# Score tiles of the four-block attention units: one accumulation chain in one pair of PSUM banks instead of two

## The chip, the cores and the metric

The kernel runs on one core of a Trainium2 chip. The metric is the device time of one execution in microseconds (us), as the median of several runs. Matmuls run on TensorE (PE, with weight loads as PEld), the other engines are VectorE (DVE), ScalarE (ACT), GpSimd (POOL) and SyncE (SP, which here issues the DMAs).

## The reference

One transformer block on x of 2 x 1024 tokens of width 512, with a modulation from a small conditioning vector. Cut to what matters here, for attention:

```python
h = _layernorm(x, axis=-1) * (1 + ca) + sa
q = (h @ Wq)   # 32 heads of 64, rotary embedding applied
k = (h @ Wk)   # 8 heads of 64, rotary embedding applied; each serves 4 query heads
v = (h @ Wv)   # 8 heads of 64
scores = einsum('bhqd,bhkd->bhqk', q, k) / sqrt(64)
scores = where(causal, scores, finfo.min)
out = einsum('bhqk,bhkd->bhqd', softmax(scores), v)
x = x + ga * (out @ Wo)
```

After it comes a second layernorm with modulation and a gated feed-forward of width 2048 with ternary weights and an RMS norm in the middle; the output is the residual sum. All arrays are float32.

## The kernel before

The kernel has four stages: projections of keys, values and queries with the rotary embedding (up to about 300 us in the profile), attention (to about 1030 us), the output projection with the second norm, and the feed-forward. To keep float32 accuracy on faster matmuls, an operand is split into a high and a low part, and a product is three matmul terms: high by high, high by low, low by high.

Attention goes by units. A unit (b, g, i) is one batch, one key head with its four query heads, and one group of 256 query rows, i from 0 to 3. There are 64 of them, and a unit has nb = 2i + 2 key blocks of 128 keys: 2, 4, 6 or 8. For each unit:

- "tops": `top_mm` multiplies queries by keys (high parts alone) into a pair of PSUM banks (`pm`), and `top_red` on DVE takes each query row's maximum (`mx`, with `mm` for the first half of long rows). The maxima go through `top_row` into `rows`.
- `score(j)`: the scores of key block j, transposed (keys on partitions), for four heads, in two halves of the PE array's rows. Each half writes a bank of its own, so a score tile takes a pair of banks (`ps_`). A block that starts a chain takes four terms: three products and one matmul of `unit` by `rows`, which subtracts the maximum. The next block of the chain doesn't start anew: it adds the products with the *step* of the keys, k[j] - k[j-1], onto the banks that still hold the scores of block j-1; three terms and no row term. It may do so only when both exponentials of block j-1 have read the banks (`es[j - 1]` among the task's `after`).
- `expo(j, half)`: ACT writes the exponentials into `e`; `causal(j)` on POOL masks the last two blocks.
- `value(j)`: PE multiplies `e` by the values into `po`. Values run in tasks of `SPAN[nb]` blocks.
- `total` on POOL or DVE adds the `e` tiles up (`acc`), `row_sum` sums over keys on PE (`pr`), and the result is inverted and multiplied in.

Keys are stored in DRAM in `ks`, their steps' high parts in `kds`; `load_k` and `load_steps` bring them into the tiles k1, k2 and k3. In `ks` the place of the low part holds, for key blocks 0 and 4, the low part of the block itself, and for the others the low part of the step. `FIRST` says which blocks start a chain, `ORDER` the order in which a unit's blocks are scored:

```python
ORDER = {2: [0, 1], 4: [0, 2, 1, 3], 6: [0, 4, 1, 5, 2, 3], 8: [0, 4, 1, 5, 2, 6, 3, 7]}
FIRST = {2: [0], 4: [0, 2], 6: [0, 4], 8: [0, 4]}
```

So a unit of four has two chains, 0-1 and 2-3, each in a pair of banks. Since block 2 starts a chain only in the units of four (in the longer units it is a step), its own low part is kept in an extra place of 128 columns at the front of `kds` and k3.

The order of the instructions on each engine is worked out when the program is built. Every piece is a task with a cost, a due time and what it waits for (`add`), and `Plan.run` lays them out one by one with a model of engines, banks and buffers. For PE it chooses among the tasks that can start now by due time, with corrections: `STICK` favours a task of the class PE is in (the classes are the tiling modes: full array, column-tiled values and row sums, row-tiled scores and tops); `LATE` puts off a task whose inputs are only just ready; a top is favoured by `BOOST` when DVE has less than `FEED` us of work ahead and put off by `DELAY` when it has more than `ENOUGH`; and when PE would leave the score class while DVE has less than `FILL` us of work ahead, a top is taken instead if one can start:

```python
key=lambda o: (o[2].due - STICK * (CLASS[o[2].mode] == CLASS[mode]) + LATE * o[1] - (o[2].feeds > 0) * (BOOST * (behind < FEED) - DELAY * (behind > ENOUGH)), o[2].n))
if mode == 3 and best[2].mode != 3 and behind < FILL:
    best = min((o for o in opts if o[0] <= start + TURN and o[2].feeds > 0), key=lambda o: (o[2].due, o[2].n), default=best)
```

`LATE` also enters the choice on the other engines. The eight PSUM banks are given out by the planner: two to each chain of scores, two to each pair of tops, one to a unit's `po`, and one each to short products. The weights' ternary quantisation (`pq` on PE, `ws`, `wr` on DVE) is spread over the attention stage as filling. In the first stage, `rope_mul` and `rope_end` form the steps of the keys and write them.

Of the kernel before, what the change touches and what calls it, by code (L numbers as in the profile page):

```python
# [9 lines left out]
F32R = mybir.dt.float32r  # L10
BF = mybir.dt.bfloat16
AF = mybir.ActivationFunctionType
ALU = mybir.AluOpType
# [4 lines left out]
B, S, E = 2, 1024, 512  # L18
# [162 lines left out]
TBEG, TEND, PER_UNIT = 300, 20.0, 0.8  # L181
VSUM, VSIGN, LAST = 9, 1, 3
TBEFORE, TGAP, TSKIP = 20, 20.0, 25.0
LEAD, SPREAD, STICK, LATE = 15, 0.6, 9, 4
ENTER, LEAVE, LOAD, AHEAD = 0.16, 0.37, 0.1, 0.25
CLASS = (0, 1, 1, 2)
TURN, SPARE = 0.05, 1.0
FEED, BOOST, ENOUGH, DELAY, FILL = 0.3, 22, 2, 8, 3.5
QT, PACE = 6, 4

@with_exitstack
def block_kernel(ctx, tc, x, wq, wk, wv, wo, wgu, wpj, cin, wmod, cos, sin, out):
    nc = tc.nc
    T = InOrder(tc, nc.tensor, True)
    V, A, P, SY = (InOrder(tc, e, False) for e in (nc.vector, nc.scalar, nc.gpsimd, nc.sync))
# [3 lines left out]
    def f32(ap):  # L199
        return ap.bitcast(F32)  # L200

    const = ctx.enter_context(tc.tile_pool(name="const", bufs=1, reuse_waits="tile"))
    dram = ctx.enter_context(tc.tile_pool(name="dram", bufs=1, space=DRAM))
# [7 lines left out]
    def stile(name):  # L211
        if plan:
            return bank(plan.given.pop(0), name)
        turn_of["s"] += 1
        return bank(turn_of["s"] % 4, name)
# [30 lines left out]

    qs = [[dram.tile([128, 2, 2, S], F32R, name=f"qs{b}_{g}") for g in range(KVH)] for b in range(B)]
    ks = [[dram.tile([128, 4, S], F32R, name=f"ks{b}_{i}") for i in range(2)] for b in range(B)]
    kds = [[dram.tile([2, 128, S // 8 * 7], F32R, name=f"kds{b}_{i}") for i in range(2)] for b in range(B)]
    vs = dram.tile([NT, KVH * D], F32, name="vs")  # L250

    def put_q(dst, rr, h, tok):
# [130 lines left out]
    first = {}  # L383
# [84 lines left out]
    def rope_end(n):  # L468
        while len(ropes) > n:
            (a, c, *steps), tok, dst = ropes.pop(0)  # L470
            rr = tp.tile([128, 4, 512], F32R, name="rr")
            for i, r in enumerate((a, c)):
                A.activation(rr[:, i, :], r, AF.Copy)
                if not steps:
                    V.tensor_tensor(rr[:, 2 + i, :], r, f32(rr[:, i, :]), ALU.subtract)
                    continue
                V.tensor_tensor(rr[:, 2 + i, 0:128], r[:, 0:128], f32(rr[:, i, 0:128]), ALU.subtract)
                f, to = (128, 512) if tok else (0, 0)
                if not tok:

                    V.tensor_tensor(r[:, 0:128].bitcast(F32R), r[:, 256:384], f32(rr[:, i, 256:384]), ALU.subtract)
                high = r[:, 128:512].bitcast(F32R)
                A.activation(high, steps[i], AF.Copy)
                V.tensor_tensor(rr[:, 2 + i, 128:512], steps[i], f32(high), ALU.subtract)
                half = [x for pair in kds for x in pair][[x for pair in ks for x in pair].index(dst)][i]
                SY.dma_start(f32(half[:, to:to + 512 - f]), f32(r[:, f:512].bitcast(F32R)))
            for h in (0, 2, 1, 3):
                if len(dst.shape) == 4:
                    put_q(dst, rr, h, tok)
                else:  # L490
                    SY.dma_start(f32(dst[:, h, tok:tok + 512]).rearrange("(c d) t -> d c t", c=4), f32(rr[h * 32:h * 32 + 32]))
# [92 lines left out]
    hs = []  # L584
# [33 lines left out]
    def pe(n):  # L618
        return n / 2400 + 0.018
# [19 lines left out]
    for g in range(KVH):  # L639
        d, due = {}, 5.2 * g  # L640
# [118 lines left out]

    B0 = 5.2 * KVH  # L760

    ORDER = {2: [0, 1], 4: [0, 2, 1, 3], 6: [0, 4, 1, 5, 2, 3], 8: [0, 4, 1, 5, 2, 6, 3, 7]}
    FIRST = {2: [0], 4: [0, 2], 6: [0, 4], 8: [0, 4]}
    due_s, t = {}, B0
    for u, (b, g, i) in enumerate(units):
        nb = 2 * i + 2
        for j in ORDER[nb]:
            due_s[(u, j)] = t
            n = 128 if j == nb - 1 else 256
            t += (3 + (j in FIRST[nb])) * pe(2 * n) + 8 * n / 2400 + 0.05  # L770
            t += (4 * sum((2 * i + s + 1) * 128 / 2400 + 0.06 for s in range(2)) + PER_UNIT) / nb
        due_s[(u, nb)] = t
    PBEG = t
# [11 lines left out]
    def attention(u):  # L785
        b, g, i = units[u]
# [14 lines left out]
        if u % NI == 0:  # L801
            kd = K[(b, g)] = {}

            def load_k(n):
                l, a = n // 2, n % 2
                if a == 0:
                    kd["k", l] = kp.tile([128, S], F32R, name=("k1", "k2")[l])
                SY.dma_start(f32(kd["k", l][a * 64:a * 64 + 64, :]), f32(ks[b][g // 4][l * 64:l * 64 + 64, g % 4, :]))

            def load_v():  # L810
                kd["vt"] = kp.tile([128, S // 128, 128], F32, name="vt")
                SY.dma_start(kd["vt"], vs[b * S:(b + 1) * S, g * 64:g * 64 + 128].rearrange("(t p) n -> p t n", p=128))

            kd["l"], before = [], K[units[u - 1][:2]]["l"] if u else []
            def load_steps(n):
                if n == 0:
                    kd["k", 2] = pp.tile([128, S // 8 * 7], F32R, name="k3", bufs=2)
                p = n % 2 * 64 + n // 2 * 32
                SY.dma_start(f32(kd["k", 2][p:p + 32, :]), f32(kds[b][g // 4][n // 2, g % 4 * 32:g % 4 * 32 + 32, :]))

            for n in range(4):
                kd["l"].append(add("S", 0.46, t0 - 26 + n, lambda n=n: load_k(n), order=kd["l"] + (held or before),
                                   takes=(("k1",), (), ("k2",), ())[n], dma=256 * KB))
            for n in range(4):
                kd["l"].append(add("S", 0.46, t0 - 22 + n, lambda n=n: load_steps(n), order=kd["l"], takes=() if n else ("k3",), dma=96 * KB))
            if g % 2 == 0:
                kd["lv"] = add("S", 0.46, t0 - 15, load_v, order=held or (K[units[u - 8][:2]]["lv"],) if u >= 8 else (), takes=("vt",), dma=512 * KB)
                kd["av"] = []
            else:
                kd["lv"] = K[(b, g - 1)]["lv"]  # L830
                kd["av"] = K[(b, g - 1)]["av"]
            kd["use"] = []
# [69 lines left out]

        def score(j):
            q0 = 128 if j == nb - 1 else 0
            first = j in FIRST[nb]
            c = max(x for x in FIRST[nb] if x <= j)
            if first:
                for hp_ in range(2):
                    d["p", c, hp_] = stile("ps_").rearrange("p (b q) -> p b q", q=256)
                ws = [kd["k", l][:, j * 128:(j + 1) * 128] for l in (0, 0)] + [kd["k", 2][:, 0:128] if j == 2 else kd["k", 1][:, j * 128:(j + 1) * 128]]  # L910
            else:
                at = j - j // 4
                ws = [kd["k", 2][:, at * 128:(at + 1) * 128]] * 2 + [kd["k", 1][:, j * 128:(j + 1) * 128]]
            terms = [(w_, d["t"][:, l]) for w_, l in zip(ws, (0, 1, 0))] + [(unit, rows[u % 2])] * first
            for n, (w_, x_) in enumerate(terms):
                for hp_ in range(2):
                    r = slice(hp_ * 64, hp_ * 64 + 64)
                    T.matmul(d["p", c, hp_][:, :, q0:], w_[r], x_[r, :, q0:], start=(n == 0 and first), stop=(n == len(terms) - 1), skip_group_check=True)

        def expo(j, hp_):  # L920
            q0 = 128 if j == nb - 1 else 0
            hs = slice(hp_ * 2, hp_ * 2 + 2)
            if hp_ == 0:
                home, tag, bufs = (gp, "eb", EL) if late_e[u, j] else (pp, "e", EB)
                d["e", j] = home.tile([128, 4, 256], F32, name="e", tag=tag, bufs=bufs)
            A.activation(d["e", j][:, hs, q0:], d["p", max(x for x in FIRST[nb] if x <= j), hp_][:, :, q0:], AF.Exp, scale=0.125)

        def causal(j):
            q0 = 128 if j == nb - 1 else 0
# [27 lines left out]
        for at, j in enumerate(order):  # L957
            n = 128 if j == nb - 1 else 256
            due = due_s[(u, j)]
            es[j] = []  # L960
            first, c = j in FIRST[nb], max(x for x in FIRST[nb] if x <= j)
            p = add("T", (3 + first) * pe(2 * n) + 0.03, due, lambda j=j: score(j), d["lq"] + kd["l"] + [row] + (cleared[1:2] if u == 0 else []) + ([] if first else es[j - 1]),
                    takes=("#", "#1") if first else (), mode=3)
            if first:
                chain[c] = p
            if late_e[u, j] or (u, j) not in early:
                p.order(opened)
            kd["use"].append(p)
# [1 line left out]
            for hp_ in range(2):  # L970
                x_ = add("A", ac(2 * n), due + 0.5 + 0.5 * hp_, lambda j=j, h=hp_: expo(j, h), (p,), order=es[j],
                         takes=() if hp_ else ("eb",) if late_e[u, j] else ("e",))
                if late_e[u, j]:
                    x_.order(opened)
                if j + 1 in FIRST[nb] or j == nb - 1:
                    chain[c].hold(("#", "#1")[hp_], x_)
                es[j].append(x_)
            ex[j] = es[j]
            if j >= nb - 2:
# [653 lines left out]
```

## Time and profile before

| | us |
|---|---|
| median of 3 runs | 1593.22 |
| lowest and highest | 1592.65, 1593.77 |
| the profiled execution | 1593.43 |
| its span in the profile | 1591.7 |

Busy time of the engines in three stretches of the span, in us:

| stretch | PE | DVE | ACT | POOL | granted clock | DMA share |
|---|---|---|---|---|---|---|
| 0 to 300 (projections) | 284.1 | 240.1 | 91.8 | 161.1 | 0.97 | 0.72 |
| 300 to 1030 (attention) | 708.7 | 593.6 | 408.9 | 478.8 | 0.99 | 0.55 |
| 1030 to 1592 (output projection, feed-forward) | 552.9 | 331.4 | 205.3 | 223.4 | 1.00 | 0.40 |

The stretches are cut by eye; tasks of neighbouring stages overlap. A matmul's end is modelled in the profile, so that records of neighbouring matmuls overlap: a busy PE need not be PE at its peak. All instructions carry the line of a helper (L39), so they are told apart by the names of what they write and read: `ps__7260<-t,k` is a score matmul into the score tile 7260, `ps__...<-row,unit` its row term, `pm` a top, `po` a value, `pr` a row sum, `pq` a ternary sum. A value or row-sum matmul (float32 operands) is recorded as two instructions.

### The profile page before, as it was taken

The numbers are of one execution on the slowest core, as the hardware profiler recorded it, in microseconds if no ns is written. First come the engines' busy times: TensorE is split into PE (matmuls) and PEld (weight loads), VectorE is DVE, ScalarE is ACT, GpSimd is POOL, SyncE is SP. The second block draws the span as 40 slices with busy tenths as digits, with TensorE's granted clock in tenths as the row PEclk, the third lists the DMA queues.
The fourth block names the chain that finished last, engine by engine and source line by source line (L and its number), as shares of the span: only waits on it lengthen the run. The fifth ranks groups of instructions, "written<-read, shape, count | busy, mean of one in ns | idle before, by whom it ended". The sixth has DMA issues, their size and how long they took to land.

```text
span 1591.7 us, 26776 instructions
## 1 busy us (share of the span) xinstructions
PE 1545.7 (97%) x9028; PEld 1068.5 (67%) x9028; DVE 1165.1 (73%) x2456; ACT 706.0 (44%) x1361; POOL 863.3 (54%) x764
## 2 busy tenths in 40 slices
PE   8899999999999999999999999999999999999998
PEld 7688887755554555555555555477787887888886
DVE  6798887787777788887878888847878675444434
ACT  3423222246555556555545656635555432222221
POOL 4365565537676676655676675713323544444443
PEclk9999999989999999999999999999999999999999
DMA  7766758775555445655546554576868733020000
GB/s 244 231 198 194 230 166 233 225 190 140 159 153 158 139 126 171 170 138 157 155 133 172 144 150 143 161 245 206 249 213 248 283 109 130 1 80 0 14 14 27
DMA packets 206593, 250.55 MB, mean 157 GB/s; under 512 B 34932, under 2 KB 144500, under 8 KB 206456
## 3 DMA queue, kind: packets, MB, share of 16 engines
q1 hardware_dynamic: 206456, 248.85, 52.6%
q8 instruction: 71, 1.16, 0.3%
q14 instruction: 66, 0.54, 0.1%
HBM read 156.24 MB, written 92.02 MB: 156 GB/s over the span
## 4 chain that ended last, share of the span: by engine, by line
PE 66%; DVE 6%; DMA 5%; issue 2%; SPq 2%; ACT 1%; POOL 1%; DVEq 0%; POOLq 0%; ACTq 0%
PE pgu L39 15%; PE po L39 13%; PE pj L39 10%; PE pfo L39 7%; PE pm L39 4%; DVE junk L39 3%; PE pr L39 3%; PE pqk L39 3%; SPq L39 2%; DMA k<-ks 2%; DMA t<-qs 1%; DVE mm L39 1%; ACT e L39 1%; PE pq L39 1%; DMA ri<-linv 1%
## 5 line engine op out<-in xcount | busy, mean ns | idle before, releaser
L39 POOL TENSOR_TENSOR acc<-acc,e 128x512 f32<-128x512 f32 x202 | 265.6, 1326 | 62.6 <-DVE acc L39 44.8
L39 PE MATMUL po<-e,vt 128*64 128x512 f32 (+1 forms) x1280 | 267.8, 557 | 4.1 <-DVE mx L39 1.8
L39 PE MATMUL pgu<-h,gu 128*128 128x512 f32 x1024 | 244.3, 391 | 0.0
L39 PEld LDWEIGHTS pgu<-h,gu 128*128 128x128 f32 x1024 | 192.0, 188 | 39.8
L39 DVE CUSTOM_DVE_ANT_0 junk<-pm,cmask,mm 128x384 bf16<-128x384 f32 (+1 forms) x256 | 174.6, 682 | 59.6 <-PE pm L39 34.7
L39 PEld LDWEIGHTS po<-e,vt 128*64 128x64 f32 x1280 | 84.0, 136 | 154.0 <-issue 122.2
L39 PE MATMUL pm<-k,t 64*128 64x384 f32 (+3 forms) x768 | 167.0, 385 | 13.6 <-DVE mx L39 5.3
L39 POOL TENSOR_SCALAR_AFFINE_SELECT e<-e 128x512 f32<-128x512 f32 x128 | 87.6, 687 | 144.7 <-ACT e L39 144.0
L39 PEld LDWEIGHTS pm<-k,t 64*128 64x128 f32 x768 | 94.1, 187 | 103.0 <-issue 31.3
L39 POOL TENSOR_TENSOR s<-hm 128x512 f32<-128x512 f32 x59 | 68.8, 1165 | 163.0 <-DVE hm L39 162.9
L39 DVE CUSTOM_DVE_ANT_0 junk<-pm,cmask 128x128 bf16<-128x128 f32 (+3 forms) x256 | 124.6, 487 | 37.8 <-PE pm L39 15.0
L39 DVE TENSOR_REDUCE mm<-pm 128x1 f32<-128x384 f32 (+2 forms) x256 | 128.4, 546 | 30.0 <-PE pm L39 29.7
L39 PE MATMUL pj<-woH,oh 128*128 128x512 f32 x512 | 142.1, 399 | 0.0
L39 POOL TENSOR_TENSOR on<-on,ri 128x512 f32<-128x512 f32 x64 | 85.8, 1342 | 65.9 <-DMA ri<-linv 65.4
L39 DVE TENSOR_TENSOR mL<-hm,mH 128x512 fp32r<-128x512 f32 x64 | 76.1, 1189 | 60.7 <-ACT mH L39 60.7
L39 DVE TENSOR_TENSOR hm<-gs,pgu 128x512 f32<-128x512 f32 x64 | 43.9, 685 | 94.1 <-PE pgu L39 89.7
L39 PEld LDWEIGHTS pj<-woH,oh 128*128 128x128 f32 x512 | 95.1, 188 | 20.9 <-issue 2.3
L39 ACT ACTIVATE mH<-hm 128x512 fp32r<-128x512 f32 x64 | 40.4, 632 | 146.0 <-PE pfo L39 133.2
L39 POOL TENSOR_TENSOR ra<-ra,rb 128x512 f32<-128x512 f32 x40 | 51.7, 1294 | 89.7 <-DVE rb L39 80.1
L39 PE MATMUL pfo<-pj,mH 128*128 128x512 f32 x256 | 100.4, 392 | 0.0
L39 PE MATMUL pfo<-pj,mL 128*128 128x512 f32 x256 | 99.7, 389 | 0.0
L39 ACT ACTIVATE on<-po 128x512 f32<-128x512 f32 x64 | 38.2, 597 | 102.5 <-POOL acc L39 44.3
(1488 smaller groups left out, 3707.8 us busy)
## 6 DMA issues: line engine op xcount, KB each, us to landing
qs<-rr SPq DMA_DIRECT2D x128, 256.0 KB
t<-qs SPq DMA_DIRECT2D x64, 512.0 KB
k<-ks SPq DMA_DIRECT2D x64, 256.0 KB
ri<-linv SPq DMA_DIRECT2D x128, 128.0 KB
os<-on SPq DMA_DIRECT2D x64, 256.0 KB
ks<-rr SPq DMA_DIRECT2D x32, 256.0 KB
w<-in_wgu SPq DMA_DIRECT2D x32, 256.0 KB
gus<-wr SPq DMA_DIRECT2D x32, 256.0 KB
```

The costliest lines, as they stand in the source:

```text
L39: ins = f(*a, **k)
```

## The change

In units of four blocks the second chain goes: blocks 0, 1, 2 and 3 are scored in this order and add up in one pair of banks; block 2 is a step like any other and has no row term. The units of two, six and eight keep their chains. With that, the extra place of block 2's low part goes from `kds` and k3 (7/8 of S columns become 3/4), as do the eight subtracts in `rope_end` that filled it. Four numbers of the planner change as well: STICK, LATE, FEED and FILL.

```diff
-LEAD, SPREAD, STICK, LATE = 15, 0.6, 9, 4
+LEAD, SPREAD, STICK, LATE = 15, 0.6, 6, 2
-FEED, BOOST, ENOUGH, DELAY, FILL = 0.3, 22, 2, 8, 3.5
+FEED, BOOST, ENOUGH, DELAY, FILL = 0.6, 22, 2, 8, 1
...
-    kds = [[dram.tile([2, 128, S // 8 * 7], F32R, name=f"kds{b}_{i}") for i in range(2)] for b in range(B)]
+    kds = [[dram.tile([2, 128, S // 4 * 3], F32R, name=f"kds{b}_{i}") for i in range(2)] for b in range(B)]
...
-                f, to = (128, 512) if tok else (0, 0)
-                if not tok:
-
-                    V.tensor_tensor(r[:, 0:128].bitcast(F32R), r[:, 256:384], f32(rr[:, i, 256:384]), ALU.subtract)
...
-                SY.dma_start(f32(half[:, to:to + 512 - f]), f32(r[:, f:512].bitcast(F32R)))
+                SY.dma_start(f32(half[:, tok // 4 * 3:tok // 4 * 3 + 384]), f32(high))
...
-    ORDER = {2: [0, 1], 4: [0, 2, 1, 3], 6: [0, 4, 1, 5, 2, 3], 8: [0, 4, 1, 5, 2, 6, 3, 7]}
-    FIRST = {2: [0], 4: [0, 2], 6: [0, 4], 8: [0, 4]}
+    ORDER = {2: [0, 1], 4: [0, 1, 2, 3], 6: [0, 4, 1, 5, 2, 3], 8: [0, 4, 1, 5, 2, 6, 3, 7]}
...
-            first = j in FIRST[nb]
-            c = max(x for x in FIRST[nb] if x <= j)
-            if first:
+            if j % 4 == 0:
                 for hp_ in range(2):
-                    d["p", c, hp_] = stile("ps_").rearrange("p (b q) -> p b q", q=256)
-                ws = [kd["k", l][:, j * 128:(j + 1) * 128] for l in (0, 0)] + [kd["k", 2][:, 0:128] if j == 2 else kd["k", 1][:, j * 128:(j + 1) * 128]]
+                    d["p", j // 4, hp_] = stile("ps_").rearrange("p (b q) -> p b q", q=256)
+                ws = [kd["k", l][:, j * 128:(j + 1) * 128] for l in (0, 0, 1)]
             else:
-                at = j - j // 4
+                at = j - 1 - j // 4
...
-                if j + 1 in FIRST[nb] or j == nb - 1:
-                    chain[c].hold(("#", "#1")[hp_], x_)
+                if j % 4 == 3 or j == nb - 1:
+                    chain[j // 4].hold(("#", "#1")[hp_], x_)
```

The left-out lines of the diff make the same replacement of `FIRST` by `j % 4` in the due times, in `expo` and where the score tasks are added, and the size of k3.

More of the change, by code (lines that the diff above doesn't have):

```diff
@@ L769, in block_kernel @@
             n = 128 if j == nb - 1 else 256
-            t += (3 + (j in FIRST[nb])) * pe(2 * n) + 8 * n / 2400 + 0.05
+            t += (3 + (j % 4 == 0)) * pe(2 * n) + 8 * n / 2400 + 0.05
             t += (4 * sum((2 * i + s + 1) * 128 / 2400 + 0.06 for s in range(2)) + PER_UNIT) / nb
@@ L816, in load_steps @@
                 if n == 0:
-                    kd["k", 2] = pp.tile([128, S // 8 * 7], F32R, name="k3", bufs=2)
+                    kd["k", 2] = pp.tile([128, S // 4 * 3], F32R, name="k3", bufs=2)
                 p = n % 2 * 64 + n // 2 * 32
@@ L904, in score @@
             q0 = 128 if j == nb - 1 else 0
-            first = j in FIRST[nb]
-            c = max(x for x in FIRST[nb] if x <= j)
-            if first:
+            if j % 4 == 0:
                 for hp_ in range(2):
-                    d["p", c, hp_] = stile("ps_").rearrange("p (b q) -> p b q", q=256)
-                ws = [kd["k", l][:, j * 128:(j + 1) * 128] for l in (0, 0)] + [kd["k", 2][:, 0:128] if j == 2 else kd["k", 1][:, j * 128:(j + 1) * 128]]
+                    d["p", j // 4, hp_] = stile("ps_").rearrange("p (b q) -> p b q", q=256)
+                ws = [kd["k", l][:, j * 128:(j + 1) * 128] for l in (0, 0, 1)]
             else:
-                at = j - j // 4
+                at = j - 1 - j // 4
                 ws = [kd["k", 2][:, at * 128:(at + 1) * 128]] * 2 + [kd["k", 1][:, j * 128:(j + 1) * 128]]
-            terms = [(w_, d["t"][:, l]) for w_, l in zip(ws, (0, 1, 0))] + [(unit, rows[u % 2])] * first
+            terms = [(w_, d["t"][:, l]) for w_, l in zip(ws, (0, 1, 0))] + [(unit, rows[u % 2])] * (j % 4 == 0)
             for n, (w_, x_) in enumerate(terms):
@@ L917, in score @@
                     r = slice(hp_ * 64, hp_ * 64 + 64)
-                    T.matmul(d["p", c, hp_][:, :, q0:], w_[r], x_[r, :, q0:], start=(n == 0 and first), stop=(n == len(terms) - 1), skip_group_check=True)
+                    T.matmul(d["p", j // 4, hp_][:, :, q0:], w_[r], x_[r, :, q0:], start=(n == 0 and j % 4 == 0), stop=(n == len(terms) - 1), skip_group_check=True)
         def expo(j, hp_):
@@ L925, in expo @@
                 d["e", j] = home.tile([128, 4, 256], F32, name="e", tag=tag, bufs=bufs)
-            A.activation(d["e", j][:, hs, q0:], d["p", max(x for x in FIRST[nb] if x <= j), hp_][:, :, q0:], AF.Exp, scale=0.125)
+            A.activation(d["e", j][:, hs, q0:], d["p", j // 4, hp_][:, :, q0:], AF.Exp, scale=0.125)
         def causal(j):
@@ L960, in attention @@
             es[j] = []
-            first, c = j in FIRST[nb], max(x for x in FIRST[nb] if x <= j)
+            first = j % 4 == 0
             p = add("T", (3 + first) * pe(2 * n) + 0.03, due, lambda j=j: score(j), d["lq"] + kd["l"] + [row] + (cleared[1:2] if u == 0 else []) + ([] if first else es[j - 1]),
@@ L964, in attention @@
             if first:
-                chain[c] = p
+                chain[j // 4] = p
             if late_e[u, j] or (u, j) not in early:
```

## The prediction

> **What bounds the kernel now.** I read the page's head first, then the busy time by stage, then the PE queue in order of time through the attention stage, then the waits.
>
> ```profile
> span 1591.7 us, 26776 instructions
> PE 1545.7 (97%) x9028; PEld 1068.5 (67%) x9028; DVE 1165.1 (73%) x2456; ACT 706.0 (44%) x1361; POOL 863.3 (54%) x764
> PE 66%; DVE 6%; DMA 5%; issue 2%; SPq 2%; ACT 1%; POOL 1%; DVEq 0%; POOLq 0%; ACTq 0%
> ```
> ```profile
> 300.00:1030.00 730.00, 708.65 (x5213) 393.63 (x5211) 593.61 (x1612) 408.89 (x844) 478.78 (x431) 0.99 0.55 155
> ```
>
> The columns of the second fence are the stretch, then busy time of PE, PEld, DVE, ACT, POOL, the granted clock, the DMA share and GB/s. PE ends the kernel (66% of the chain), and in the attention stage, 300 to 1030 us, it looks 97% busy while DVE is at 594 of 730 us and DMA at 55%. But the end of a matmul's record is modelled (0.39 us for 512 columns), so I counted by starts. Back to back, a pair of 64x512 score matmuls (the two halves run side by side) starts every 0.23 us (638.77 to 639.00 below; 0.2275 over longer runs); sixteen value records take 3.16 us (631.58 to 634.74), 0.1975 each; eight row-sum records take 0.46 us. With these prices the stage's records come to 286 us of scores and tops, 226 of values, 53 of row sums and 17 of full-array matmuls, 582 of 730 us. So about 148 us of the stage is PE time lost between instructions, some 105 of them in the 131 stretches of scores and tops. The change works on that pool, and on the 582.
>
> ```profile
> 629.82 0.49 PE L39 MATMUL ps__7260<-t,k 64*128 64x512 f32 x1
> ...
> 630.62 0.39 PE L39 MATMUL ps__7260<-row,unit 64*128 64x512 f32 x1
> ...
> 630.85 0.80 PE L39 MATMUL pm<-k,t 64*128 64x384 f32 x2
> 631.58 3.23 PE L39 MATMUL po<-e,vt 128*64 128x512 f32 x16
> 634.74 0.50 PE L39 MATMUL pm<-k,t 64*128 64x512 f32 x2
> 635.07 0.28 PE L39 MATMUL ps__7260<-t,k 64*128 64x256 f32 x1
> ...
> 635.65 0.40 PE L39 MATMUL ps__7336<-t,k 64*128 64x512 f32 x1
> ...
> 636.81 0.39 PE L39 MATMUL ps__7364<-t,k 64*128 64x512 f32 x1
> ...
> 637.79 0.39 PE L39 MATMUL ps__7365<-row,unit 64*128 64x512 f32 x1
> 638.11 0.39 PE L39 MATMUL pq<-wabs,gones 128*128 128x512 bf16 x1
> 638.43 0.49 PE L39 MATMUL ps__7336<-t,k 64*128 64x512 f32 x1
> ...
> 639.00 0.39 PE L39 MATMUL ps__7337<-t,k 64*128 64x512 f32 x1
> 639.23 0.67 PE L39 MATMUL pm<-k,t 64*128 64x512 f32 x2
> 639.45 0.45 PE L39 MATMUL ps__7364<-t,k 64*128 64x256 f32 x2
> ```
>
> This is PE's timeline: start, duration, out<-in. A unit of two blocks (7260) and then one of four (7336 and 7364). The unit of two has one pair of banks: block 0 at 629.82, and block 1 only at 635.07, because its matmuls add onto banks that ACT must first have read; PE fills the link with a top and a value task. The unit of four starts block 0 at 635.65, block 2 on a second pair at 636.81, block 1 at 638.43, block 3 at 639.45: while ACT reads one pair, PE writes the other.
>
> ```profile
> 637.27 0.59 ACT L39 ACTIVATE e<-ps__7337 128x512 f32<-128x512 f32 x1
> ```
> ```profile
> PE pm L39 <- DVE mx L39: 5.3, 17, 0.5
> PE pr L39 <- DVE mx L39: 2.4, 8, 0.5
> ```
>
> The first line is ACT's: block 0's second exponential ends at 637.86, 1.5 us after block 0's last matmul started at 636.35, and that 1.5 is about the median over all scores. The waits view (engine waiting, releaser, us, times, longest) shows little idle time in the attention stage, and most of it waits for DVE's row maxima to give banks back; all waits for mx and mm together are about 12 us.
>
> **Matmuls removed.** In the 16 units of four, block 2 becomes a step instead of a start and drops its row-unit pair (637.56 and 637.79 above). 16 x 0.2275 = 3.6 us, off PE, the bound: -3.6.
>
> **First stage and DMA.** Eight 128x128 subtracts leave DVE (0.29 to 1.20 us each, 4.8 in all, at 34 to 45 and 185 to 193 us). There DVE still sits idle 4.24 us before 57.31, and from 176 to 216 us PE is busy in every slice, so PE covers them: 0. Were they on the path, -4.8. The step loads shrink from 112 to 96 KB and eight step stores from 256 to 192 KB, same counts and queue (SP), in stages with DMA at 40 to 72%: 0, and no PE wait names kds.
>
> **The links.** Now a unit of four runs 0, 1, 2, 3 on one pair. Each of blocks 1, 2 and 3 waits for both exponentials of the block before; PE's queue is in order, so what stands behind such a block would wait too, unless other work is put ahead. The shortest link in the trace is 1.9 to 2.0 us start to start, of which a step's own matmuls take 0.69 (638.43 to the top, less the gap), so a link leaves 1.3 us to be filled. Three links in 16 units are 62 us of filling that the second pair used to give. If nothing covered them: +62. If all is covered: 0, for the units of two, which live on such a link already, lose 13% of their span by the same count (0.74 of 5.5 us), the longer units 15 to 18%. I take the nearer row, the unit of two: the link is covered by a trip to a value task or a row sum. What costs is the trip. PE takes 0.32 us from a score to a ternary matmul and 0.32 back, against 0.22 to 0.23 within a mode, so 0.10 each way. The stage makes 91 visits to values, nearly one for each of the kernel's 96 value tasks, and 58 to row sums, so most trips are made anyway; I charge one more per unit of four: 16 x 0.20 = +3.2. The last blocks' masks on POOL (0.65 us each) now fall together at the end, ahead of the unit's value task, which other units' scores cover.
>
> **The planner's constants.** STICK 9 to 6 and LATE 4 to 2 let PE leave a class of work when another is 6 us overdue instead of 9. Only neighbours can be parted: 37 times a row sum and a value task stand side by side now. All parted, at 0.20 a trip: +7.4; none: 0; I take half, +3.7. FILL 3.5 to 1 asks for 1 us of queued DVE work, not 3.5, before PE leaves scores and tops. Today 75 of 131 such stretches end in a top, 29 of them in two to four; the surplus over one is 43 tops, each with two reductions of 0.55 to 0.75 us and their read-outs, about 1.4 us of DVE work. That is 60 us of DVE work that may no longer lie under a value task, where DVE already idles 56 us over 91 visits. If it is only idle time moved, 0; at worst PE waits for all of it, +60. I scale the existing waits: DVE's idle time in the stage, 137 us, grows by 60, or 44%; the same share of PE's 12 us of waits for maxima is 5, and I take 6, since tops moved to a later stretch also find fewer free banks. FEED 0.3 to 0.6 works against it, calling a top sooner when DVE runs dry: half of it back, +3. If FEED wins outright, the 12 us of waits go: -12.
>
> **A rule weighed.** The row above has 0.10 us for a switch between score and ternary matmuls. The Trainium skill, "TensorEngine Tiling (Array Packing)", section Tiling Modes, says that changing the tiling mode, as against the tile, drains TensorE; that speaks against a change that makes PE leave row-tiled work more often. If a drain meant waiting out the last matmul's whole record, 0.39 less 0.23 us, or 0.16 a switch, then by this estimate from the rule the trips of both parts (6.9 us at 0.10) would be 11.0, and the sum 4.1 higher. The trace has the duration, so 0.10 is used.
>
> **Sum.** -3.6 + 0 + 3.2 + 3.7 + 3.0 = +6.3 us on the profiled execution's 1593.43 (span 1591.7 and 1.7 around it, 0.2 above the median of 1593.22): 1599.7, or 1599.5 on the median's scale.
>
> **Rivals.** *Slower, the forecast* (0.55): links are covered, but by more trips and with DVE fed later: 1596.5 to 1609. *Faster* (0.22): the links need no trip of their own, as in the units of two, and FEED keeps DVE supplied so that waits for maxima shrink by half (-6): -3.6 - 6 gives about 1584 to 1590, say 1586; if only the trips vanish and DVE stays as it is, -3.6, 1589.6. For it: PE is the bound, the matmuls are really gone, DVE has 137 us idle. Against it: the pool of 148 us needs to grow by only 2.5% to eat the gain. It decides where the pool grows by less than 3.6 us. *Same* (0.13): trips and DVE cost just what the 16 pairs save, 1590 to 1596.4. *Links laid bare* (0.10): a third of the 62 us is not covered, since the next units need banks (eight, of which a pair of tops takes two, a value sum one) to have scores ready; +21 on top of the rest but the trips: 1609 to 1630. The waits view speaks against it: today one wait of 0.4 us is put down to an exponential.
>
> **Chances and range.** Measured runs lie within 0.04% of one another; 0.2%, 3.2 us, is about what can be told from no change. Faster 0.22, same 0.13, slower 0.65. The range of 8 in 10 runs from 1587 (leaving out 0.10 of the faster case) to 1609 (leaving out the bare links); the forecast's own is 1596.5 to 1609.
>
> **What would show it.** Score records down from 2144 (320 blocks of 3 terms and 112 row terms, two halves each) to 2112, and PE time by starts 3.6 us lower: the first term. Units of four spread over about 12 us (three links near the 4 us median) instead of 8.2, with value tasks or row sums between their blocks: the links. More than 302 stretches of one mode between 300 and 1030 us: the trips. Fewer tops at the end of a stretch and more than 56 us of DVE idle under value tasks: FILL. I am wrong if the stage gets shorter, or if PE's waits for e reach tens of us; the later stages, where PE is in one mode and full, should keep their length.

## Result and the profile after

The changed kernel took 1602.9 us in the median of five runs (1601.03 to 1608.95), against 1593.77 for the kernel before: ratio 1.0057, interval 1.004 to 1.0073. A second series gave 1607.1 against 1594.77, ratio 1.0071 (1.0056 to 1.0086). So it is slower by 9 to 12 us. The kernel before is less steady than the three runs known at first: 23 runs of it in one series span 1590.91 to 1599.07, 0.5%, not the 0.04% that the prediction went by. The first profiled execution lay at 1608.95, 6 us over its own median; the readings below are from the second series' profile, at 1607.71.

The page of the changed kernel (second series):

```profile
span 1606.0 us, 26731 instructions
PE 1554.5 (97%) x8996; PEld 1067.2 (66%) x8996; DVE 1156.0 (72%) x2448; ACT 708.1 (44%) x1361; POOL 864.8 (54%) x764
PE 65%; DVE 8%; DMA 5%; SPq 2%; issue 2%; ACT 1%; POOL 0%; DVEq 0%; ACTq 0%
```

32 matmuls are gone (9028 to 8996) and eight DVE instructions, as the change says; the share of PE in the chain is one point lower, that of DVE two higher. The attention stage by windows, columns as before:

```profile
300.00:1030.00 730.00, 702.44 (x5092) 384.93 (x5092) 590.58 (x1616) 402.85 (x825) 478.20 (x427) 1.00 0.54 153
```

PE starts 121 fewer records in the same 730 us (5213 before), more than the 32 that were removed: the stage is behind, not merely lighter. A unit of four in PE's timeline:

```profile
647.90 0.39 PE L39 MATMUL ps__7342<-t,k 64*128 64x512 f32 x1
...
648.61 0.38 PE L39 MATMUL ps__7342<-row,unit 64*128 64x512 f32 x1
...
648.83 0.41 PE L39 MATMUL pm<-k,t 64*128 64x512 f32 x2
649.16 0.64 PE L39 MATMUL pr<-e,ones 128*32 128x256 f32 x8
649.62 0.61 PE L39 MATMUL pr<-acc,ones 128*32 128x256 f32 x8
650.17 0.49 PE L39 MATMUL ps__7341<-t,k 64*128 64x512 f32 x1
...
651.66 0.38 PE L39 MATMUL pm<-k,t 64*128 64x256 f32 x1 [0.20 <-DVE mx L39]
652.67 1.51 PE L39 MATMUL po<-e,vt 128*64 128x512 f32 x8 [0.62 <-DVE mx L39]
654.11 0.86 PE L39 MATMUL pr<-e,ones 128*32 128x256 f32 x16
...
655.12 0.39 PE L39 MATMUL ps__7341<-t,k 64*128 64x512 f32 x1
...
655.91 0.39 PE L39 MATMUL pq<-wabs,gones 128*128 128x512 bf16 x1
656.23 0.44 PE L39 MATMUL pm<-k,t 64*128 64x384 f32 x2
656.57 0.50 PE L39 MATMUL ps__7478<-t,k 64*128 64x512 f32 x1
...
657.95 0.40 PE L39 MATMUL ps__7341<-t,k 64*128 64x256 f32 x2
```

Blocks 0, 1, 2, 3 start at 647.90, 650.17, 655.12 and 657.95, on one pair of banks. Tops stand in every link, with row sums in the first, values and row sums in the second, and a ternary sum and another unit's scores (7478) in the third. Over all 16 units of four, from the first score to the last exponential's end, the mean went from 8.2 to 11.5 us, and PE's lost time inside it (by starts, priced as in the prediction) from 1.2 to 3.0 us a unit. The growth of 1.8 us overstates the cost: a unit that is spread over more time also takes in more of what the stage loses anyway (148 of 730 us before), and 16 times 1.8 us is 29, while the stage grew by 10. From 300 to 1030 us PE makes 316 stretches of one mode, not 302, and DVE idles 65 us under value tasks, not 56.

The waits of PE in the whole kernel:

```profile
PE pm L39 <- DMA t<-qs: 6.0, 1, 6.0
PE pm L39 <- DVE mx L39: 5.9, 16, 0.7
...
PE po L39 <- DVE mx L39: 3.9, 8, 0.9
```

The first line is new in size. It is the first top of attention, whose queries land at about the same time as before (1.5 us later, counted from the modulation matmuls of the table below), but PE now has it in its queue ahead of twelve query matmuls (three rows of four) that used to come first. The changed kernel, then the kernel before:

```profile
270.18 1.07 PE L39 MATMUL pqk<-hH,wqL 128*128 128x512 f32 x4
277.22 0.44 PE L39 MATMUL pm<-k,t 64*128 64x128 f32 x1 [5.98 <-DMA t<-qs]
```
```profile
270.18 1.07 PE L39 MATMUL pqk<-hH,wqL 128*128 128x512 f32 x4
...
272.90 1.07 PE L39 MATMUL pqk<-hH,wqL 128*128 128x512 f32 x4
275.70 0.32 PE L39 MATMUL pm<-k,t 64*128 64x128 f32 x1 [1.74 <-DMA t<-qs]
```

Before, the same wait was 1.7 us. In all nine profiles with the old STICK and LATE it is 1.7 to 2.6 us, in all five with the new ones 5.4 to 6.0.

**One table for all runs.** To place the loss I cut every profile at four starts: the modulation matmuls in the first stage at about 125 us (they move by some 9 us between executions, and the matmuls ahead of them stand in the same order in every kernel), the first score, the last score and the last output projection. What follows the last projection is 357.8 us to the last matmul in nearly every kernel (357.5 in two).

| kernel (chains in units of four, constants) | ratio | modulation to first score | first to last score | last score to last projection |
|---|---|---|---|---|
| before (two, old) | 1 | 188.3 | 718.0 | 195.8 |
| changed (one, new), second series | 1.0071 | 193.1 | 728.0 | 195.3 |
| e1 (two, new) | 1.0112 | 192.6 | 721.4 | 210.2 |
| e2 (one, old) | 1.0096 | 188.5 | 727.4 | 204.5 |
| e3 (two, FEED and FILL new) | 1.0088 | 190.1 | 719.2 | 208.5 |
| e4 (two, STICK and LATE new) | 1.0109 | 191.4 | 719.8 | 209.1 |
| e5 (two, scored in order, old) | 1.0129 | 189.3 | 724.0 | 211.5 |
| e6 (two, old, row pair left out) | 1.0009 | 187.6 | 719.9 | 195.9 |
| n3 (two, old, LEAD 15.3) | 1.0078 | 188.2 | 718.2 | 209.9 |
| n4 (one, new, LEAD 15.3) | 1.0013 | 192.5 | 721.4 | 196.8 |
| x1 (n3, late loads moved) | 1.0036 | 189.5 | 720.1 | 201.2 |
| x3 (two, old, short maxima) | 0.9946 | 188.5 | 709.4 | 195.8 |
| x4 (two, old, third term left out) | 0.9987 | 189.2 | 715.1 | 197.6 |

The ratios come from many runs, the stages from one profile each. Two profiles with the same order up to the end of attention (n3 and x1; the changed kernel twice) differ by 2 us between first and last score; that is the grain of the table.

### The profile page after: what moved, and what is told of

Read it like the earlier page. It is cut to its first block, busy times and chain, and to the rows that moved or that the text cites. A ratio compares the mean times of both kernels' runs of the same rounds, so it can differ in the third digit from the quotient of the medians.

```text
span 1607.2 us, 26731 instructions
## 1 busy us (share of the span) xinstructions
PE 1555.4 (97%) x8996; PEld 1064.9 (66%) x8996; DVE 1154.5 (72%) x2448; ACT 708.8 (44%) x1361; POOL 865.2 (54%) x764
## 4 chain that ended last, share of the span: by engine, by line
PE 65%; DVE 7%; DMA 5%; SPq 2%; issue 2%; ACT 1%; POOL 1%; DVEq 0%; POOLq 0%; ACTq 0%
PE pgu L39 14%; PE po L39 13%; PE pj L39 10%; PE pfo L39 7%; PE pm L39 4%; DVE junk L39 3%; PE pqk L39 3%; SPq L39 2%; PE pr L39 2%; DMA k<-ks 1%; DMA t<-qs 1%; DMA k<-kds 1%; DVE ws L39 1%; DVE mm L39 1%; DVE acc L39 1%
## 5 line engine op out<-in xcount | busy, mean ns | idle before, releaser
L39 PE MATMUL pm<-k,t 64*128 64x384 f32 (+3 forms) x768 | 174.7, 388 | 18.8 <-DVE mx L39 6.2
L39 POOL TENSOR_TENSOR sq<-sq,s 128x512 f32<-128x512 f32 x59 | 80.5, 1364 | 4.5
```

Source lines behind the costliest of these rows:

```text
L39: ins = f(*a, **k)
```

## Experiments

**The change cut in four: e1 to e4.**

e1, the two chains with all four new constants:

```diff
-LEAD, SPREAD, STICK, LATE = 15, 0.6, 9, 4
+LEAD, SPREAD, STICK, LATE = 15, 0.6, 6, 2
-FEED, BOOST, ENOUGH, DELAY, FILL = 0.3, 22, 2, 8, 3.5
+FEED, BOOST, ENOUGH, DELAY, FILL = 0.6, 22, 2, 8, 1
```

> The kernel before (two chains in the units of four) with all four new constants. Theory of the prediction: the constants cost +3.7 (STICK, LATE) and +3 (FEED, FILL), so 1600.5, ratio 1.004, and more than 302 stretches of one mode in the attention stage. Rival 'the chain alone': the constants only suit the chain and cost nothing by themselves, ratio 0.999 to 1.001. Rival 'the constants are all of it': ratio 1.008, since the 16 row pairs are still there.

Measured 1613.53 against 1594.15: 1.0112 (1.0092 to 1.0133), worse than the whole change. None of the three ratios expected holds; the stretches of one mode do exceed 302 (312).

e2, the changed kernel with the two lines of constants set back.

> The changed kernel with the four constants of before. Theory of the prediction: -3.6 for the row pairs and +3.2 for the trips of the links, so 1593.5, ratio 1.000, and the units of four spread over 11 to 12 us. Rival 'the chain alone': ratio 1.006, like the whole change. Rival 'the constants are all of it': 1590, ratio 0.998.

Measured 1609.79: 1.0096 (1.0075 to 1.0117). Again worse than the whole change, and outside all three expectations. The units of four spread over 12.4 us, about as expected, but PE makes fewer stretches of one mode than before, 285 for 302, so more trips can't be what the chain costs.

e3 has only the second line of e1's edit, e4 only the first.

> The kernel before with FEED 0.6 and FILL 1 alone. Theory of the prediction: +3 us, ratio 1.002, with more DVE idle time under value tasks than 56 us. Rival 'FEED wins': down to -12 us, ratio 0.993 to 0.999. Rival 'FILL lays DVE bare': +10 us or more, ratio 1.006 and up.

Measured 1608.99: 1.0088 (1.0067 to 1.0109). The number lies in the last rival's range, but not in its place: DVE idles 62 us under value tasks for 56, attention is as long as before within the grain (719.2 for 718.0), and the loss lies behind it.

> The kernel before with STICK 6 and LATE 2 alone. Theory of the prediction: +3.7 us, ratio 1.002, with 10 to 20 more stretches of one mode and fewer row sums next to value tasks than 37. Rival 'nothing is parted, the tasks are visited one by one already': ratio 1.000. Rival 'work is taken before its input is there': a longer wait for the first queries at 275 us (1.7 us before, 5.5 in the changed kernel's profile), ratio 1.002 from that place alone.

Measured 1611.67: 1.0109 (1.009 to 1.0127). The last rival of e4 is there in part: the wait for the first queries is 5.5 us, and modulation to first score is 191.4 against 188.3. It is also there in e1 (5.4) and in the changed kernel, and not in e2 (1.9): it belongs to STICK and LATE. The rest of e4's loss is elsewhere. The forecast parting is small: 32 neighbours of row sum and value task for 37, and 298 stretches, not more than 302.

So each half of the change costs 15 us or more by itself and both together 9 to 12. The table says why they don't add: in the attention stage they nearly do (+3.4 for the constants, +9.4 for the chain, +10 for both), but e1 to e4 lose another 9 to 14 us *behind* it, which the whole change doesn't. That suggested a new theory: the planner's order is fragile, and anything that makes it lay out the work anew hits or misses stalls at places that have nothing to do with the edit.

**Order alone and two nudges: e5, n3, n4; the row pair alone: e6.**

```diff
-    ORDER = {2: [0, 1], 4: [0, 2, 1, 3], 6: [0, 4, 1, 5, 2, 3], 8: [0, 4, 1, 5, 2, 6, 3, 7]}
+    ORDER = {2: [0, 1], 4: [0, 1, 2, 3], 6: [0, 4, 1, 5, 2, 3], 8: [0, 4, 1, 5, 2, 6, 3, 7]}
```

> The kernel before, two chains in the units of four, but scored 0, 1, 2, 3 (old constants). Theory 'links': the two chains no longer cover each other, but each has one link only and the pair of block 2 is free at once, so it lies between before and the one chain with old constants (1.0096): 1.003 to 1.007. Theory 'picked order', formed after the first four runs: the order that the planner gives before is an uncommonly good one, and any change that makes it lay out the work anew costs 10 to 18 us, whatever it means: 1.007 to 1.012.

e5 measured 1615.24 against 1594.59: 1.0129 (1.0107 to 1.0151), above both expectations, with an interval that overlaps the second. By the table, 6 us of it lie in attention and 16 behind it.

n3 and n4 change one number in the kernel before and in the changed one:

```diff
-LEAD, SPREAD, STICK, LATE = 15, 0.6,
+LEAD, SPREAD, STICK, LATE = 15.3, 0.6,
```

> The kernel before with LEAD 15.3 in place of 15: the tops fall due 0.3 us earlier, which by itself should mean nothing. Theory 'each constant has its own cost': within 2 us of before, 0.999 to 1.001. Theory 'picked order': +8 to +18 us, 1.005 to 1.011, with new waits in other places, some of them after the attention stage.

> The changed kernel with LEAD 15.3 in place of 15. Theory 'each constant has its own cost': like the changed kernel, 1.0057. Theory 'picked order': the changed kernel's order was picked as well, so 1.007 to 1.014.

n3: 1607.63, 1.0078 (1.0058 to 1.0098), with attention as short as before (718.2) and 14 us lost behind it. n4: 1596.47, 1.0013 (1.0002 to 1.0025): the same nudge made the changed kernel *faster*, by 6.6 us in attention. "Picked order" fits the kernel before, and fails for the changed one, whose order was no uncommonly good one; "each constant has its own cost" fails for both. With LEAD 15.3 in both kernels the sign turns: 1.0013 with one chain, 1.0078 with two.

e6 drops the row pair without touching the plan:

```diff
-            terms = [...] + [(unit, rows[u % 2])] * first
+            terms = [...] + [(unit, rows[u % 2])] * (first and j % 4 == 0)
```

> The kernel before with the row pair of block 2 left out in the 16 units of four when the matmuls are emitted; the planner's order and the other instructions stay as they are (the maximum is then not subtracted in blocks 2 and 3 of these units). Theory of the prediction: PE is the bound, so -3.6 us, ratio 0.998. Theory 'DVE or the planned order holds PE anyway': 0.999 to 1.000.

Measured 1596.53: 1.0009 (0.9997 to 1.002). The second theory holds: 32 matmuls less at the same order gain nothing, and the forecast 0.998 lies outside the interval.

**What paces attention: x3 and x4; the handover: x1; the change again: x2.**

```diff
-            terms = [(w_, d["t"][:, l]) for w_, l in zip(ws, (0, 1, 0))] + ...
+            terms = [(w_, d["t"][:, l]) for w_, l in zip(ws[:2], (0, 1, 0))] + ...
```

> The kernel before with the third product of every score (low part of the keys by high part of the queries) left out at emission; order and all other instructions stay. That takes 320 pairs, some 66 us of starts, off PE in the attention stage. Theory 'PE bounds the stage': -50 to -66 us, ratio 0.959 to 0.969. Theory 'removed matmuls leave their time as a wait for the next exponential or bank', which the left-out row pairs suggest (3.6 us off, 0 gained): -10 to -30 us, ratio 0.981 to 0.994.

Measured 1591.68 against 1594.77: 0.9987 (0.9972 to 1.0002). Both theories asked for more: 66 us of PE starts were taken away, and attention is 3 us shorter. Its windows and longest wait:

```profile
300.00:1030.00 730.00, 684.07 (x4581) 344.53 (x4579) 600.18 (x1616) 407.34 (x847) 480.90 (x432) 0.98 0.56 155
```
```profile
PE pm L39 <- DVE mx L39: 12.1, 38, 0.9
```

632 fewer matmul records in the window, and the other engines stand where they stood (DVE 600 us for 594). PE waits for the maxima twice as long as before (12.1 us for 5.3), and still reads as 94% busy. The granted clock of the stretch is 0.98 for 0.99, worth up to some 7 us of PE, so a small part of the 66 went there.

```diff
-                V.tensor_reduce(dst, pm[:, :w], AX.X, ALU.max)
+                V.tensor_reduce(dst, pm[:, :128], AX.X, ALU.max)
```

> The kernel before with the maximum of a long row's first half taken over 128 keys in place of 384 or 512; order and all other instructions stay (softmax does not depend on the value that is subtracted). That takes 128 x 0.26 + 64 x 0.40 = some 59 us off DVE in the attention stage, 594 of 730 us. Theory 'PE bounds the stage, as the prediction said': 0 to -5 us, ratio 0.997 to 1.000. Theory 'DVE's maxima, which give banks back, set the pace': -20 us and more, ratio below 0.988.

Measured 1585.99: 0.9946 (0.9931 to 0.9962), attention 8.6 us shorter:

```profile
300.00:1030.00 730.00, 710.23 (x5262) 397.29 (x5264) 540.32 (x1626) 411.12 (x850) 483.43 (x434) 0.99 0.56 157
```

(The window reaches past x3's last score, so some later work of DVE is in its 540 us.) That is between the two expectations: of some 59 us taken off DVE, 8.6 come back as time; of 66 taken off PE, 3. So DVE's maxima are nearer to the pace than PE's matmuls, and neither alone is the pace at this order. x3 is faster than both kernels, at a price: what is subtracted is no longer the row's maximum, so an exponential may exceed one, which a kernel for wider scores could not allow.

x1 starts from n3 and adds one order:

```diff
+        d["rt"] = rt
...
-        start, after = ([opened], []) if g < HELD else ([staging], [projecting])
+        start, after = ([opened], []) if g < HELD else ([staging] + [w["rt"] for w in U[-4:]], [projecting])
```

> The kernel before with LEAD 15.3, and the eight late loads of the output projection's weights put behind the last units' row-sum turns in SP's queue; up to there the order is that of before with LEAD 15.3 (1.0078). Theory 'handover': that kernel loses nothing in the attention stage but 14 us behind it, because these loads (5.7 us of SP) stand ahead of the last units' small transfers, so the late weights are converted 5 us too late, PE waits, and its clock is held back after the wait; with the loads moved the waits for woH go, and the ratio falls to 1.000 to 1.003. Theory 'the attention stage's order is what costs': no change, 1.007 to 1.009.

Measured 1600.26: 1.0036 (1.0016 to 1.0056), 7 us better than n3; the ratio lies a little above the expected band, its interval overlaps it. Last score to last projection fell from 209.9 to 201.2 us. SP's queue in n3, where the weight loads stand ahead of two of the last units' small transfers, and in x1:

```profile
1050.90 5.71 SPq L39 DMA_DIRECT2D oacc<-in_wo  x8
1056.77 0.33 SPq L39 DMA_DIRECT2D linv<-l  x1
1057.45 0.60 SPq L39 DMA_DIRECT2D l<-ls  x1
```
```profile
1052.81 0.59 SPq L39 DMA_DIRECT2D linv<-l  x1
1053.50 0.59 SPq L39 DMA_DIRECT2D l<-ls  x1
1054.14 4.22 SPq L39 DMA_DIRECT2D oacc<-in_wo  x8
```

and PE's waits between 1030 and 1260 us, n3 and then x1:

```profile
PE pt L39 <- DVE xr L39: 4.2, 4, 2.7
PE pj L39 <- ACT woH L39: 1.5, 2, 1.0
```
```profile
PE pt L39 <- DVE xr L39: 1.6, 3, 0.6
...
PE pj L39 <- DVE woL L39: 0.2, 1, 0.2
```

The last units' normalisation ends later when its small transfers wait behind the loads; until it has ended, the late weights of the output projection may not be converted; and PE, having used up what it holds, waits for woH and then for the second norm's xr. With the loads behind, the waits for woH go and those for xr shrink to 1.6 us, and with the waits of n3 goes the time for which its clock was withheld (last section). Two limits: the planner lays out what stands behind the loads anew, so that x1 differs from n3 there in more than their place, and x1's 201.2 us are still 5.4 more than before, for which no cause was tried. In e1, e2 and e3 the same waits for woH stand in the trace, and in e2, e4 and e5 single waits of 2.4 to 5.2 us for wabs, in e5 3.2 for oh, in e1 and e3 4.4 and 2.4 for POOL's acc, at the same place; there the cause was read, not tried.

x2 is the changed kernel again.

> The changed kernel once more, for a profile nearer to its median (the first lies 6 us above it). Ratio 1.0057 as before. Theory 'the chain costs in the attention stage': first to last score 725 to 730 us, against 718.0 in before, with the stretch of the output projection (first to last pj) as before, 189 to 192 us. Theory 'the first profile's attention stage is only a disturbed one': 718 to 721 us, and the loss lies in front of the first score.

Measured 1607.1: 1.0071 (1.0056 to 1.0086). Attention 728.0 us, last score to last projection as before (first to last projection 188.6 us, just under the expected band): the first theory holds for this order; n4 shows one chain with 721.4.

## Why the prediction was right or wrong

The sign and the size held (1599.5 forecast, 1602.9 and 1607.1 measured, both in the range), but by luck: hardly any term held, a part of +4.8 us was missing, and the sign itself hangs on LEAD, a number that the change doesn't touch (n3, n4).

- *What bounds the kernel.* This step failed. PE ends the chain and is full outside attention, but inside it PE is not the pace: x4 took off 66 us and the stage gave back 3. The 148 us of "lost" time were counted rightly and read wrongly, as overhead that PE adds to its work. By the same count the time lost between first and last score grew from 148 to 211 us in x4: what was taken off came back nearly whole as lost time. How much of the 148 is waiting already, and how much the switching between modes, no run shows.
- *Row pairs, -3.6.* e6 gained nothing (+1.4 us, between -0.5 and +3.2), for that reason.
- *Links, +3.2.* Right on what happens to the unit, wrong on the price, and two to three times too small. With old constants the chain costs 9.4 us between first and last score (e2 against before), with the new ones 6.6 (the changed kernel against e1). The units spread to 11.5 us, as forecast ("about 12"), and cover was there, as forecast. What failed is the price by trips: with the chain alone (e2) PE makes 17 fewer stretches of one mode and the stage is 9.4 us longer, and n4, with the most stretches (323), has 721.4. What the runs show in its place is PE time lost inside the unit (1.2 to 3.0 us, part of it not the chain's), which the prediction put at nothing because the units of two live on a link already. n4 warns against taking the price as fixed: one chain, and only 3.4 us more than before.
- *STICK and LATE, +3.7.* In attention, new constants cost 3.4 us with two chains (e1) and 0.6 with one (the changed kernel against e2), all four together, where +6.7 was forecast; these are near the grain of 2 us. In the changed kernel 25 neighbours of row sum and value are left of 37, 12 parted for the forecast 18, but STICK and LATE alone (e4) part 5.
- *FEED and FILL, +3.* Stretches that end in exactly one top went from 46 to 69, those with more stayed at 28 or 29, and the surplus over one fell only from 43 tops to about 32. DVE's idle time under values grew by 9 us, not by up to 60. With the two constants alone (e3) the surplus falls further, to about 19, and still attention is within the grain of before: moving tops costs nothing that these runs can tell.
- *Missing: the first score.* +4.8 us, of which 4.2 are a wait that the prediction did not look at: LATE and STICK bring the first top ahead of query products while its queries are still on the way.
- *Later stages keep their length.* True for the change (195.3 for 195.8), but by luck, and not for the reason given, that PE is in one mode and full there: e1 to e5 and n3 lose 9 to 16 us between the last score and the last projection.
- *Same-sized pieces add up.* The prediction summed four terms. Measured, the chain alone costs 1.0096, the constants alone 1.0112, both 1.0057 to 1.0071. The whole comes to +4.8 before the first score, +10 in attention and -0.5 behind it.

What is left open: what does set the pace of attention at a given order. DVE's maxima have a part in it (8.6 us for 59); the rest may be the round trips from PE to ACT or DVE and back, which is an idea that no run tried. No run took ACT's or POOL's work away. And with one nudge to each kernel, the runs can't say what one chain costs apart from the order that the planner happens to find.

## What to carry to other kernels

An engine that ends the chain and reads 97% busy may still not be the pace of a stage: take a large piece of its work away at an unchanged order and see what comes back before a removed instruction is priced at its duration. Where a planner lays out in-order queues, a constant moves the whole order, so compare a change with what a meaningless nudge of the same planner does (here 12 us slower for one kernel, 6 to 11 us faster for the other) before its effect is put down to its meaning. And a long run of loads that becomes ready at once, put ahead of a few small transfers in one queue, can cost as much behind the stage (7 us here) as a change of order inside it.

## What the runs showed of the hardware

PE's clock was withheld after waits of less than 3 us. In n3, after the wait of 2.7 us at 1112 to 1115 us, projection matmuls ran at half their pace for some 5 us (four in 2.06 us by the record, 1.07 later on):

```profile
1115.41 0.48 PE L39 MATMUL pt<-ident,xr 128*128 128x128 f32 x1 [2.71 <-DVE xr L39]
1116.31 1.76 PE L39 MATMUL pt<-ident,xr 128*128 128x128 f32 x7 [0.42 <-DVE xr L39]
1117.71 2.06 PE L39 MATMUL pj<-woH,oh 128*128 128x512 f32 x4
...
1126.97 1.07 PE L39 MATMUL pj<-woH,oh 128*128 128x512 f32 x4
```
The windows view of n3 and of x1 for 1110 to 1150 us; the granted clock is the third number from the end:

```profile
1110.00:1150.00 40.00, 35.82 (x154) 27.91 (x153) 29.70 (x56) 23.23 (x46) 16.94 (x18) 0.91 0.76 239
```
```profile
1110.00:1150.00 40.00, 38.26 (x174) 30.07 (x172) 34.37 (x63) 22.81 (x44) 15.33 (x16) 1.00 0.77 244
```

At 0.91, about 3.5 of the 40 us are withheld, more than the wait itself; x1, with waits of at most 0.6 us there, keeps the full clock. The kernel before shows it too: after the waits of 1.74 us at 274 to 276 us and of 0.75 us just behind, its granted clock is 0.51 from 276 to 283 us, while after one wait of 1.55 us at 651 us it stays at 1.00. The Trainium skill, "TensorE: Matmul & The Clock Gate", Part 1, has the clock fall back after an idle window of about 3.4 us; here no single wait at these places was longer than 2.71 us, and the measurement decides.
